# A mixture-of-experts block on one core: the down projection of 25 experts rewritten from eight passes of full width into seven products of half width

## The chip, the core and the metric

The kernel runs on one core of a Trainium2 chip. TensorE (PE in the profile; PEld is its weight load) multiplies matrices into PSUM. VectorE (DVE), ScalarE (ACT) and GpSimd (POOL) do elementwise work. SyncE (SP) issues most DMAs; POOL issues the indirect ones (gathers and scatters by index). The engines run at the same time and wait for one another through semaphores; each works through its own list strictly in the order in which the program wrote it. The metric is the device time of one execution in microseconds (us).

## The reference, cut to what matters

The input is 8 x 1024 tokens of 512 numbers, all in f32. Each token is normalised; one branch is a gated recurrence over time, the other a shared feed-forward block plus 32 routed experts, of which each token uses one. The part that the change touches is the routed branch:

```python
topk_ids = jnp.argmax(logits, axis=-1)
xs = x * scores
sorted_x = xs[order]                       # tokens grouped by expert
g = grouped_mm(sorted_x, routed_gate_w)    # 512 -> 1024, per expert
u = grouped_mm(sorted_x, routed_up_w)      # 512 -> 1024
d = grouped_mm(silu(g) * u, routed_down_w) # 1024 -> 512
out = x + s * silu(shared_out + d[inv])
```

## The kernel before

**Two phases.** The first (to about 2787 us in the profile) runs the recurrence and the shared block over 16 chunks of 512 tokens, with large products in Strassen's form, and routes the tokens. Its last part, the drain, runs only the output projections (L1055). The second phase runs the 32 experts one after the other. Experts are sorted by their number of tokens; the one at place e has a fixed number of slots, `WIDTHS[e]`, from 376 down to 224 (25 of them have 248 or more). Tokens beyond the slots would go to a loop after the experts (L1533), of which the profile has no row.

**One expert** is a `Chunk` (L170). Its slots lie in 2 or 3 tiles of 128 tokens. `gather_in` (L200) fetches token rows with indirect DMAs on POOL, four of 32 rows a tile; `transpose` (L229) turns them on DVE into `xsT`. `compute` (L253) runs over eight blocks j of the hidden size. Per j it does 4 matmuls for g and 4 for u (L272), the sigmoid on ACT (L277), two multiplications on DVE (L279, L280) that give `h`, and then `down` of the block before (L261): 4 matmuls of the full width, which add into four PSUM banks `accs` over all eight j. So gate and up of block j, and down of block j - 1, alternate on PE. At the end DVE transposes the banks (L299) into `yT`.

**What follows an expert** is done during the next one: `store` and `fetch` (L304, L315) take `yT` through DRAM on SP; `gather_rest` (L219) fetches the rows of the other branches; `bias`, `sums` and `finish` (L345, L322, L350) combine them on DVE and ACT; a scatter on POOL writes the output (L360).

**Order.** The order on each engine is written by hand: `between[j]` (L1496 to L1519) lists what is issued after block j. A `gather_in` or weight load of expert e + 2 stands in expert e.

```python
if e + 2 < E:
    between[3 if e == 0 else 1].append(lambda: chunks[e + 2].weight("g"))
    between[2].append(chunks[e + 2].gather_in)
...
between[6].append(chunk.gather_rest)
if e + 2 < E:
    between[7] += [lambda q=q: chunks[e + 2].weight(q) for q in "ud"]
```

**Buffers.** Each weight matrix (2 MB) takes one of NW = 7 buffers in turn (L369). `alloc2` (L376) gives the others: 6 tiles of gathered rows, 3 of `h`, 5 of `rest`. g and u share 4 PSUM buffers, so g of block j + 2 takes the place of g of block j once DVE has read it. The first expert's three matrices are loaded during the drain, each in one DMA, at its start and at steps 10 and 20 (L1460, L1471).

Of the kernel before, what the change touches and what calls it, by code (L numbers as in the profile page):

```python
# [8 lines left out]
FP = mybir.dt.float32  # L9
I32 = mybir.dt.int32  # L10
AF = mybir.ActivationFunctionType
ALU = mybir.AluOpType
# [5 lines left out]
P = 128  # L18
T = 512
NT = T // P  # L20
BL = 32
NA = P // BL
C = 384
CT = C // P
# [9 lines left out]
def tile_kernel(  # L34
# [45 lines left out]
    nc = tc.nc  # L80
    B, S, H = x.shape
    N = B * S
    DI = init_h.shape[0]
    E, _, I = rgate_w.shape
    KH = H // P
    NJ = DI // P
    NI = I // P
# [20 lines left out]
    def work(name):  # L108
        return pools["work"].tile([P, 512], FP, tag="w", name=name)

    pools = {}
# [8 lines left out]
        out=upper, in_=ones, pattern=[[1, P]], compare_op=ALU.is_gt, fill=0.0,  # L120
# [49 lines left out]
    class Chunk:  # L170
# [6 lines left out]
        def __init__(self, alloc, alloc_w, name, cols, fours, width, w_src, whole=False, direct=True):  # L177
            self.whole = whole
            self.direct = direct
            self.alloc, self.alloc_w, self.name, self.w_src = alloc, alloc_w, name, w_src  # L180
            self.width, self.cols, self.fours = width, cols, fours
            self.wt, self.src = [], None
            self.tiles = [
                (t, min(P, width - t * P)) for t in range(-(-width // P))
            ]

        def weight(self, tag):
            q = "gud".index(tag)
            w = self.alloc_w([P, KH * I], f"{self.name}_w{tag}")
            w = w.rearrange("p (k f) -> p k f", k=(KH, KH, NI)[q])  # L190
            self.src = self.src or self.w_src()
            rows = "(k p) f -> p k f" if tag == "d" else "(p k) f -> p k f"
            nc.sync.dma_start(out=w, in_=self.src[q].rearrange(rows, p=P))
            self.wt.append(w)

        def weights(self):
            for tag in "gud":
# [55 lines left out]
        def compute(self, between):  # L253


            wg, wu, wd = self.wt
            xsT, alloc, name, W = self.xsT, self.alloc, self.name, self.width

            def down(j, h):
                for m in range(KH):  # L260
                    nc.tensor.matmul(  # L261
                        accs[m][:, :W], lhsT=wd[:, j, m * P : (m + 1) * P], rhs=h[:, :W],
                        start=(j == 0), stop=(j == NI - 1),
                    )

            last = None
            for j in range(NI):
                g = work(f"{name}_g{j}")
                u = work(f"{name}_u{j}")
                for o, w in ((g, wg), (u, wu)):  # L270
                    for k in range(KH):
                        nc.tensor.matmul(  # L272
                            o[:, :W], lhsT=w[:, k, j * P : (j + 1) * P], rhs=xsT[:, k, :W],
                            start=(k == 0), stop=(k == KH - 1),
                        )
                sig = alloc([P, C], "sig", f"{name}_sig{j}")
                nc.scalar.activation(sig[:, :W], g[:, :W], AF.Sigmoid)  # L277
                h = alloc([P, C], "h", f"{name}_h{j}")
                nc.vector.tensor_tensor(sig[:, :W], sig[:, :W], g[:, :W], ALU.mult)  # L279
                nc.vector.tensor_tensor(h[:, :W], sig[:, :W], u[:, :W], ALU.mult)  # L280
                if last is not None:
                    down(*last)
                last = (j, h)
                for step in between.get(j, ()):
                    step()
            down(*last)
            if self.direct:
                self.yT = alloc([P, KH, C], "yT", f"{name}_yT")
                for m in range(KH):
                    if m % 2:  # L290
                        nc.vector.tensor_copy(self.yT[:, m, :W], accs[m][:, :W])
                    else:
                        nc.scalar.copy(self.yT[:, m, :W], accs[m][:, :W])
                return

            nb = -(-W // BL)
            self.yT = alloc([P, C // BL, KH, BL], "yT", f"{name}_yT")
            for m in range(KH):
                nc.vector.transpose(  # L299
                    self.yT[:, :nb, m, :],  # L300
                    accs[m][:, : nb * BL].rearrange("p (b c) -> p b c", c=BL),
                )

        def store(self):  # L304

# [60 lines left out]
    accs = []  # L366
    ydram = [dram.tile([C, H], FP, name=f"ydram{q}") for q in range(3)]
    yturn = iter(range(E))
    NW = 7  # L369
    turn = iter(range(3 * E))  # L370

    def alloc_w(shape, name):
        i = next(turn) % NW
        return pools["wa" if i < 4 else "wb"].tile(shape, FP, tag=f"w{i}", name=name)

    def alloc2(shape, tag, name):  # L376
        bufs = {"xs": 2 * CT, "xsT": 2, "sig": 2, "h": 3, "y": 3, "s": 2, "yT": 2, "rest": CT + 2}
        pool = pools["in" if tag in ("xs", "xsT") else "by"]
        return pool.tile(shape, FP, tag=tag, name=name, bufs=bufs[tag])

    chunks = [
        Chunk(
            alloc2, alloc_w, f"e{e}",
            lambda t, e=e: pools["idx"][:, e * CT + t : e * CT + t + 1],
            lambda t, b, e=e: pools["fours"][:, b, e * CT + t : e * CT + t + 1],
            WIDTHS[e], lambda e=e: expert(eid[0:1, e : e + 1]), e == 0, e == E - 1,
        )
        for e in range(E)
    ]
# [23 lines left out]
    op = c1.enter_context(tc.tile_pool(name="op", bufs=1))  # L413
# [12 lines left out]
    steps = {}  # L426
# [582 lines left out]
    for c in range(NCHUNK):  # L1009
        g = SC * (c + 1)  # L1010
# [368 lines left out]
    d = Dispatch()  # L1379
# [10 lines left out]
    last = SC * (NCHUNK - 1)  # L1390
# [38 lines left out]
    for now in range(END):  # L1429
        name, back = ORDER[now % 7]  # L1430
        n = now // 7 - back
# [25 lines left out]
    pools["far"] = c1.enter_context(tc.tile_pool(name="far", bufs=2, side="right"))  # L1457
    for _ in range(2):
        out_fetch()
    chunks[0].weight("g")  # L1460
    k = 0
    while filled < 2 * NCHUNK * PER:
        now += 1
        for step in steps.pop(now, ()):
            step()
        while filled < due(now):
            next(fill)
            filled += 1
        k += 1
        if k in (10, 20):  # L1470
            chunks[0].weight("ud"[k // 20])  # L1471
        if filled >= 2 * NCHUNK * PER - 24 and "xsT" not in vars(chunks[0]):
            pools["work"] = ps_w
            for t in range(CT):
                chunks[0].transpose(t)
# [11 lines left out]
    for m in range(KH):  # L1487
        acc = pools["acc"].tile([P, H], FP, tag="acc", name=f"acc{m}")
        nc.vector.memset(acc, 0.0)
        accs.append(acc)  # L1490
    with ExitStack() as c3:
        pools["wb"] = c3.enter_context(tc.tile_pool(name="wb", bufs=1, reuse_waits="tile"))
        pools["by"] = c3.enter_context(tc.tile_pool(name="by", bufs=2, reuse_waits="tile"))
        chunks[1].gather_in()
        for e, chunk in enumerate(chunks):
            between = {j: [] for j in range(NI)}  # L1496
            if e:
                before = chunks[e - 1]
                between[0].append(before.store)
                between[1].append(before.fetch)  # L1500
                for t in range(CT):
                    between[1 + t].append(lambda t=t: before.bias(t))
                    between[3 + t].append(lambda t=t: before.sums(t))
                    between[4 + t].append(lambda t=t: before.finish(t))
            if e == 0:
                for j, tag in enumerate("gud"):
                    between[j].append(lambda tag=tag: chunks[1].weight(tag))
            if e + 2 < E:
                between[3 if e == 0 else 1].append(lambda: chunks[e + 2].weight("g"))
                between[2].append(chunks[e + 2].gather_in)  # L1510
            if e + 1 < E:
                for t in range(CT):
                    between[5 + t].append(lambda t=t: chunks[e + 1].transpose(t))
            between[6].append(chunk.gather_rest)
            if e + 2 < E:
                between[7] += [lambda q=q: chunks[e + 2].weight(q) for q in "ud"]
            if e == E - 1:
                for t in range(CT):
                    between[7].append(lambda t=t: chunk.bias(t))  # L1519
            chunk.compute(between)  # L1520
        for t in range(CT):
            for step in (chunks[-1].sums, chunks[-1].finish):
                step(t)
# [4 lines left out]
    with tc.tile_pool(name="wo", bufs=3) as wo, tc.tile_pool(name="so", bufs=3) as so:  # L1528
        n = nc.values_load(
            nov[0:1, 0:1], min_val=0, max_val=MAXOV,  # L1530
            skip_runtime_bounds_check_because="a sum of at most MAXOV comparisons of counts that sum to N",
        )
        with tc.For_i(0, n, 1) as i:  # L1533
# [5 lines left out]
            def alloc(shape, tag, name):  # L1539
                return so.tile(shape, FP, tag=tag, name=name)  # L1540
# [48 lines left out]
```

## Time and profile before

| what | value |
|---|---|
| median of 3 runs | 4257.02 us (4255.71 to 4257.21) |
| profiled execution | 4237.99 us, of it the span 4236.3 us |
| granted TensorE clock, mean | 0.997 |
| experts 0 to 24 (2786.8 to 3950.8 us): PE busy | 1164.0 of 1164.0 us |
| same stretch: DVE, ACT, POOL busy | 506.5, 122.8, 370.1 us |
| same stretch: DMA engines' mean busy share | 0.65 |
| DVE's waits for the y rows fetched from DRAM | 23.7 us in 19 waits, longest 2.4 |
| DVE's waits for the gathered rest rows | 1.5 us, one wait |

A row of the profile names the line, the engine, the operation and what is written from what; numbers in tile names are left out, so all experts share a row. An f32 matmul is two instructions in the trace, with a weight load (PEld) each. Matmuls are pipelined: the duration of one includes its way through the array, so the distance from start to start, not the duration, tells the rate. Timeline rows give the start, the length, the engine, and in brackets the idle time before and what ended it.

### The profile page before, as it was taken

The numbers are of one execution on the slowest core, as the hardware profiler recorded it, in microseconds if no ns is written. First come the engines' busy times: TensorE is split into PE (matmuls) and PEld (weight loads), VectorE is DVE, ScalarE is ACT, GpSimd is POOL, SyncE is SP. The second block draws the span as 40 slices with busy tenths as digits, with TensorE's granted clock in tenths as the row PEclk, the third lists the DMA queues.
The fourth block names the chain that finished last, engine by engine and source line by source line (L and its number), as shares of the span: only waits on it lengthen the run. The fifth ranks groups of instructions, "written<-read, shape, count | busy, mean of one in ns | idle before, by whom it ended". The sixth has DMA issues, their size and how long they took to land.

```text
span 4236.3 us, 51931 instructions
## 1 busy us (share of the span) xinstructions
PE 4198.9 (99%) x18719; PEld 3527.2 (83%) x18719; DVE 2083.9 (49%) x3425; ACT 1978.0 (47%) x3577; POOL 1105.3 (26%) x1182
## 2 busy tenths in 40 slices
PE   9999999999999999999999999999999999999998
PEld 4688888888888888888888888866777788889998
DVE  5555555544554545555545456424444444544444
ACT  5676676666666766666767666501111111111110
POOL 3222122111221121212211225442232333323221
PEclk9999999999999999999999999999999999999999
DMA  8767666666676666766666656575666567677773
GB/s 277 244 214 231 207 216 216 210 223 206 213 226 216 217 213 203 231 202 216 222 210 220 214 177 205 179 267 181 211 227 226 205 236 242 222 253 242 243 263 113
DMA packets 506854, 925.61 MB, mean 218 GB/s; under 512 B 38397, under 2 KB 324509, under 8 KB 498402
## 3 DMA queue, kind: packets, MB, share of 16 engines
q1 hardware_dynamic: 478754, 831.89, 59.2%
q0 software_dynamic: 27840, 90.36, 6.4%
q8 instruction: 150, 2.46, 0.2%
q14 instruction: 110, 0.90, 0.1%
HBM read 805.27 MB, written 134.92 MB: 222 GB/s over the span
## 4 chain that ended last, share of the span: by engine, by line
PE 97%; DVE 1%; DMA 1%; issue 0%; ACT 0%; POOL 0%; SPq 0%; POOLq 0%; ACTq 0%
PE b L759 24%; PE u L1055 18%; PE c L759 12%; PE e_u L272 11%; PE e_g L272 11%; PE acc L261 11%; PE a L759 6%; PE b L710 3%; PE lgp L520 0%; DMA e_xs<-rec,idx 0%; PE lgt L530 0%; PE b L725 0%; DMA x<-in_L_attn_x_dram 0%; DMA e_rest<-rec,idx 0%; POOL s L1007 0%
## 5 line engine op out<-in xcount | busy, mean ns | idle before, releaser
L759 PE MATMUL b<-t,sums 128*128 128x256 f32 x2400 | 616.1, 379 | 1.2 <-DVE t L681 1.2
L1055 PE MATMUL u<-wP,s 128*128 128x256 f32 x2032 | 598.4, 380 | 6.1 <-issue 6.1
L277 ACT ACTIVATE e_sig<-e_g 128x280 f32<-128x280 f32 (+15 forms) x256 | 101.8, 398 | 931.8 <-PE e_g L272 931.6
L272 PE MATMUL e_u<-e_xsT,e_wu 128*128 128x296 f32 (+15 forms) x2048 | 518.0, 396 | 0.0
L272 PE MATMUL e_g<-e_xsT,e_wg 128*128 128x296 f32 (+15 forms) x2048 | 518.0, 396 | 0.0
L261 PE MATMUL acc<-e_h,e_wd 128*128 128x296 f32 (+15 forms) x2048 | 512.8, 396 | 0.0
L759 PEld LDWEIGHTS b<-t,sums 128*128 128x128 f32 x2400 | 454.8, 190 | 63.0 <-ACT a L773 1.3
L272 PEld LDWEIGHTS e_g<-e_xsT,e_wg 128*128 128x128 f32 x2048 | 389.1, 190 | 87.2
L272 PEld LDWEIGHTS e_u<-e_xsT,e_wu 128*128 128x128 f32 x2048 | 389.1, 190 | 87.1
L261 PEld LDWEIGHTS acc<-e_h,e_wd 128*128 128x128 f32 x2048 | 389.1, 190 | 87.1
L1055 PEld LDWEIGHTS u<-wP,s 128*128 128x128 f32 x2032 | 387.2, 191 | 61.1 <-issue 8.3
L279 DVE TENSOR_TENSOR e_sig<-e_sig,e_g 128x280 f32<-128x280 f32 (+15 forms) x256 | 113.1, 442 | 481.6 <-ACT e_sig L277 481.2
L213 POOL DMA_INDIRECT e_xs<-rec,fours x276 | 262.4, 951 | 178.2 <-DMA e_rest<-rec,idx 86.0
L759 PE MATMUL c<-xnT,sums 128*128 128x256 f32 x1200 | 308.0, 379 | 0.0
L759 PE MATMUL c<-t,sums 128*128 128x256 f32 x1200 | 308.0, 379 | 0.0
L759 PE MATMUL b<-xnT,nat 128*128 128x256 f32 x1200 | 308.0, 379 | 0.0
L759 PE MATMUL a<-xnT,nat 128*128 128x256 f32 x1200 | 308.0, 379 | 0.0
L759 PE MATMUL b<-t,nat 128*128 128x256 f32 x1200 | 308.0, 379 | 0.0
L360 POOL DMA_INDIRECT out_dram<-e_rest,idx x84 | 93.1, 1109 | 801.2 <-DVE e_rest L359 798.2
L759 PEld LDWEIGHTS b<-xnT,nat 128*128 128x128 f32 x1200 | 228.0, 190 | 31.4 <-issue 0.5
L759 PEld LDWEIGHTS a<-xnT,nat 128*128 128x128 f32 x1200 | 228.0, 190 | 31.0
L759 PEld LDWEIGHTS c<-t,sums 128*128 128x128 f32 x1200 | 228.0, 190 | 31.0
(243 smaller groups left out, 6381.2 us busy)
## 6 DMA issues: line engine op xcount, KB each, us to landing
sums<-sdram SPq DMA_DIRECT2D x300, 512.0 KB, 4.6
nat<-in_L_attn_W_dram SPq DMA_DIRECT2D x192, 512.0 KB, 4.6
e_wg<-L_ffn_routed_gate_w_dram SPq DMA_DIRECT2D x32, 2048.0 KB, 8.4
e_wu<-n_L_ffn_routed_up_w_dram SPq DMA_DIRECT2D x32, 2048.0 KB, 12.7
e_wd<-L_ffn_routed_down_w_dram SPq DMA_DIRECT2D x32, 2048.0 KB, 19.0
wP<-tdram SPq DMA_DIRECT2D x127, 512.0 KB, 3.5
nat<-L_ffn_shared_gate_w_dram SPq DMA_DIRECT2D x64, 512.0 KB, 4.9
nat<-n_L_ffn_shared_up_w_dram SPq DMA_DIRECT2D x64, 512.0 KB, 4.3
```

Of the source, the lines that this page charges most:

```text
L213: nc.gpsimd.indirect_dma_start(out=r[:, b, :], out_offset=None, in_=rec1.rearrange("n (a d) -> (n a) d", a=NA), in_offset=bass.IndirectOff ...
L261: nc.tensor.matmul(accs[m][:, :W], lhsT=wd[:, j, m * P : (m + 1) * P], rhs=h[:, :W], start=(j == 0), stop=(j == NI - 1),)
L272: nc.tensor.matmul(o[:, :W], lhsT=w[:, k, j * P : (j + 1) * P], rhs=xsT[:, k, :W], start=(k == 0), stop=(k == KH - 1),)
L277: nc.scalar.activation(sig[:, :W], g[:, :W], AF.Sigmoid)
L279: nc.vector.tensor_tensor(sig[:, :W], sig[:, :W], g[:, :W], ALU.mult)
L360: store = nc.gpsimd.indirect_dma_start(out=of[:, :], out_offset=bass.IndirectOffsetOnAxis(ap=col[:n, :], axis=0), in_=o, in_offset=None, b ...
L710: nc.tensor.matmul(ps[:, part], lhsT=natural[n][:, k, block * P : (block + 1) * P], rhs=xnTs[0][:, k, part], start=(k == 0), stop=(k == KH ...
L759: nc.tensor.matmul(ps, lhsT=lhs[:, k, :], rhs=rhs[:, k, :], start=(new and k == 0), stop=(k == KQ - 1),  skip_group_check=True,)
L1055: nc.tensor.matmul(ps[:, q, :], lhsT=lhs[:, q * P : (q + 1) * P], rhs=w[:, p, :],  start=(q == 0 and p == 0 and name in ("P1", "P2", "P5") ...
```

## The change

For experts with 248 slots or more (and not the last), `down` moves out of the loop over j. The eight `h` blocks are kept in one tile `hid`, and after gate and up of all eight blocks `down_fast` multiplies the 1024 x 512 weights with it in Strassen's form (Winograd's variant): both are cut into four quarters and seven products of quarters replace eight. Each product is 8 matmuls of half the width. The sums of weight quarters (`weight_sum`, 4 of 1024 columns) and of hidden quarters (`down_sum`, 4 of half the width times 4) are new on DVE; ACT copies three intermediate results out of PSUM, DVE adds three, and the result is transposed from a tile `o` in SBUF. The next expert's transposes of its second and third tile move from j = 6, 7 to after the fifth product's eviction, the first to j = 2.

Other edits: weights g and u of expert e + 2, its gather, and then `gather_rest` are issued at j = 7; weight d of expert e + 1 at j = 0, between `store` and `fetch`. The first expert's weights come in four parts of 256 hidden columns, two in the drain (steps 8 and 24), two at j = 0 and 1. NW is 6; there are 3 tiles of gathered rows and 3 of `rest`.

```diff
+            self.fast = not direct and width >= 248
...
+        def quarter(self, q):
+            if q == 0:
+                for tag in "gud":
+                    self.weight(tag, load=False)
+            n, k = I // 4, NI // 4
+            for i, w in enumerate(self.wt[:2]):
+                nc.sync.dma_start(
+                    out=w[:, :, q * n : (q + 1) * n],
+                    in_=self.src[i][:, q * n : (q + 1) * n].rearrange("(p k) f -> p k f", p=P),
+                )
...
+            hid = self.hid = alloc([P, NI, C], "hid", f"{name}_hid")
...
-                if last is not None:
-                    down(*last)
-                last = (j, h)
+                if j and not self.fast:
+                    down(j - 1)
+                if j == NI - 2 and self.fast:
+                    self.down_sum(1)
...
+            if self.fast:
+                self.down_fast(between.get("down", ()))
+            else:
+                down(NI - 1)
...
+        def weight_sum(self, q):
...
+            l, r, op = {
+                1: (A21, A22, ALU.add), 2: (S[:, 0], A11, ALU.subtract),
+                3: (A11, A21, ALU.subtract), 4: (A12, S[:, 1], ALU.subtract),
+            }[q]
+            nc.vector.tensor_tensor(S[:, q - 1], l, r, op)
...
+        def down_fast(self, steps):
+            W, h = self.width, self.width // 2
+            for q in (2, 3):
+                self.down_sum(q)
...
+            for name, ps, lhs, rhs in (
+                ("P1", chain, self.down_part(0, 0), lambda: self.hidden_part(0, 0)),
+                ("P5", side, S[:, 0], lambda: T[1]),
+                ("P6", chain, S[:, 1], lambda: T[2]),
+                ("P2", other, self.down_part(0, 1), lambda: self.hidden_part(1, 0)),
+                ("P7", chain, S[:, 2], lambda: T[3]),
+                ("P3", side, S[:, 3], lambda: self.hidden_part(1, 1)),
+                ("P4", chain, self.down_part(1, 1), lambda: T[4]),
+            ):
+                rhs = rhs()
+                for q in range(2):
+                    for j in range(NI // 2):
+                        nc.tensor.matmul(
+                            ps[:, q * h : (q + 1) * h], lhsT=lhs[:, j, q * P : (q + 1) * P],
+                            rhs=rhs[:, j, :],
...
+                if name == "P1":
+                    evict("a1", ps)
+                elif name == "P5":
+                    evict("b5", ps)
+                    self.down_sum(4)
+                    for step in steps:
+                        step()
...
-    NW = 7
+    NW = 6
...
-        bufs = {"xs": 2 * CT, "xsT": 2, "sig": 2, "h": 3, "y": 3, "s": 2, "yT": 2, "rest": CT + 2}
+        bufs = {"xs": CT, "xsT": 2, "sig": 2, "y": 3, "s": 2, "hs": 2, "rest": CT}
...
-        if k in (10, 20):
-            chunks[0].weight("ud"[k // 20])
+        if k in (8, 24):
+            chunks[0].quarter(k // 24)
...
+    pools["o"] = osb.tile([P, KH, C], FP, name="o")
+    nc.gpsimd.memset(pools["o"], 0.0)
...
+            for q in range(1, 5):
+                between[q + 2 if e == 0 else q - 1].append(lambda q=q: chunk.weight_sum(q))
+            if 0 < e < E - 1:
+                between[0].append(lambda: chunks[e + 1].weight("d"))
             if e + 1 < E:
                 for t in range(CT):
-                    between[5 + t].append(lambda t=t: chunks[e + 1].transpose(t))
-            between[6].append(chunk.gather_rest)
+                    step = (2, "down", "down")[t] if chunk.fast else 5 + t
+                    between.setdefault(step, []).append(lambda t=t: chunks[e + 1].transpose(t))
             if e + 2 < E:
-                between[7] += [lambda q=q: chunks[e + 2].weight(q) for q in "ud"]
+                between[7] += [lambda q=q: chunks[e + 2].weight(q) for q in "gu"]
+                between[7].append(chunks[e + 2].gather_in)
+            between[7].append(chunk.gather_rest)
```

## The prediction, made before the changed kernel ran

> **What bounds the kernel now.** I read the page from the top: busy shares, the slices, then the chain of waits.
>
> ```profile
> PE 4198.9 (99%) x18719; PEld 3527.2 (83%) x18719; DVE 2083.9 (49%) x3425; ACT 1978.0 (47%) x3577; POOL 1105.3 (26%) x1182
> ...
> PE   9999999999999999999999999999999999999998
> ...
> PEclk9999999999999999999999999999999999999999
> ...
> PE 97%; DVE 1%; DMA 1%; issue 0%; ACT 0%; POOL 0%; SPq 0%; POOLq 0%; ACTq 0%
> ```
>
> TensorE (PE) is on the chain for 97% of the span, at full clock. A busy PE need not be a PE at its rate, so I went to its timeline inside the second phase, for an expert of 272 slots:
>
> ```profile
> 3487.27 2.00 PE L272 MATMUL e_g<-e_xsT,e_wg 128*128 128x272 f32 x8
> 3489.11 2.00 PE L272 MATMUL e_u<-e_xsT,e_wu 128*128 128x272 f32 x8
> ...
> 3494.61 2.00 PE L261 MATMUL acc<-e_h,e_wd 128*128 128x272 f32 x8
> ```
>
> Each f32 matmul is two records, so 4 matmuls show as x8. Starts are 1.835 us apart: 229.3 ns a record. Expert 0 (376 slots) begins at 2786.79 and expert 1 at 2847.43: 60.64 us for 192 records, 315.8 ns each. Both fit (columns / 1.2 + 2.5) ns. With it the 25 experts of 248 slots or more (widths sum to 7200) take 192 x (6000 + 25 x 2.5) ns = 1164.0 us; the trace has expert 25 start at 3950.79, 1164.00 us after 2786.79. PE has no gap there: what saves PE records saves time, and any wait put before PE costs in full.
>
> **The records saved.** Down was 64 records of the full width W. Strassen has 7 products x 8 matmuls = 112 records of W/2. In W, 64W/1.2 - 56W/1.2 = 6.67W ns is saved, less 48 x 2.5 = 120 ns: 1.69 us at W = 272. Over 25 experts 48.0 - 3.0 = 45.0 us, if 124 to 188 columns keep the same rule. No row has such a matmul with these operands, and PEld speaks against it:
>
> ```profile
> L261 PEld LDWEIGHTS acc<-e_h,e_wd 128*128 128x128 f32 x2048 | 389.1, 190 | 87.1
> ```
>
> If a load's 190 ns were its pitch, 112 records would take 21.3 us at every width: 25 x 21.3 = 532 us against 64 x (6000 + 62.5) ns = 388 us now, 144 us lost. The Trainium skill, "TensorE: Matmul & The Clock Gate", section LDWEIGHTS, prices a load at columns/1.2, 107 ns for 128. Two small places decide: a pair of loads with little to hide behind, and four transposes of 128 columns.
>
> ```profile
> 2520.70 0.29 PEld L1205 LDWEIGHTS terms<-terms,ones 32*128 32x128 f32 x2 [0.33 <-issue]
> ```
>
> ```profile
> 416.48 0.60 PE L530 MATMUL lgt<-ident,lgT 128*128 128x128 f32 x4
> 416.92 0.81 PE L759 MATMUL b<-t,sums 128*128 128x256 f32 x3
> ```
>
> The two loads, 0.18 us each, fit into 0.29: the second starts 0.11 after the first. The four transposes, each with its own load, start 0.11 apart, which is 128/1.2 + 2.5. So 190 is a latency and about 108 ns the floor. The same page's section "Back-to-back issue gap" says more against the change: sustained pairs at 128 columns take about 81 ns where the plain formula gives 56, 25 ns more. By that rule 2800 records x 25 ns = 70 us would turn 45 saved into 25 lost. The transposes show no such excess, and I take the trace. Only 124 columns (105.8 ns) fall under 108: 3 experts x 112 x 2.7 ns = 0.9 us. **Saved on PE: 44.1 us** (1164.0 to 1119.9). The seven products wait on other engines; a satisfied wait costs nothing in the present rows.
>
> **DVE, the engine that must now keep up.** Gate and up no longer have down between them: a step j lasts 16 records, 3.67 us at 272, where it was 5.50. These are DVE's intervals now:
>
> ```profile
> 3511.31 0.44 DVE L280 TENSOR_TENSOR e_h<-e_sig,e_u 128x272 f32<-128x272 f32 x1 [0.47 <-PE e_u L272]
> 3511.66 0.68 DVE L357 TENSOR_TENSOR e_rest<-e_rest 128x512 f32<-128x512 f32 x1
> 3512.38 0.69 DVE L358 TENSOR_TENSOR e_rest<-e_rest,e_s 128x512 f32<-128x512 f32 x1
> 3513.11 0.69 DVE L359 TENSOR_TENSOR e_rest<-e_rest 128x512 f32<-128x512 f32 x1
> 3513.71 0.69 DVE L339 TENSOR_TENSOR e_rest<-e_y,e_rest 128x512 f32<-128x512 f32 x1
> ```
>
> Start to start: the pair of mults 0.79, 512 columns 0.60, finish 0.72 + 0.73 + 0.60 = 2.05, a transpose 1.09. New: a weight sum of 1024 columns, nearest row L905 (1214 ns), and a hidden sum of 4 x 136 = 544, 0.73 from the 512 row. With them:
>
> - j2: 0.79 + bias 0.60 + weight sum 1.21 + transpose 1.09 = 3.69
> - j3: 0.79 + sums 0.60 + bias 0.60 + weight sum 1.21 = 3.20
> - j4 and j5: 0.79 + finish 2.05 + sums 0.60 = 3.44 each
> - j6: 0.79 + hidden sum 0.73 + finish 2.05 = 3.57
>
> 17.3 us of DVE in 18.3 of PE. At 264, the tightest, 17.2 in 17.8. DVE just fits. Call the end of u7 T. DVE does the last mult and the second hidden sum by about T + 1.4; P1 and P5 (32 records of 115.8 ns) cover until T + 3.7, where P6 needs that sum. So a lag of DVE up to **2.3 us is free**; beyond that PE stands. P4 needs P7's add, with P3 (1.85 us) as cover for 0.6: free. Evictions by ACT (0.4 us each, ACT at a tenth here) are covered by the product between. The fourth hidden sum waits for P5; behind it on DVE stand two transposes for the next expert, done by T + 6.3, needed at T + 13.
>
> **Queues that are moved.** POOL: the gather of e+2 now stands at j7 ahead of gather_rest, and its second tile waits for those transposes. At 1.25 us a gather, rest0 is issued at T + 12.1. DVE wants it (bias in j1, behind it all of j2) at about T + 20.8. Landing has these bounds: 5.1 us with no weights under way (last expert, 4207.34 to 4212.45) and
>
> ```profile
> e_rest<-rec,idx POOLq DMA_INDIRECT x84, 10.9
> ```
>
> with 4 MB of weights beside it. Here gate and up (4 MB) start at T and are nearly through at T + 13, so I take 7 to 8: no stall; both ends stay inside the free lag (10.9 gives a lag of 2.2).
> SP: weight d (2 MB) now stands between the y stores and the y fetch. Without weights yT to landing took 6.2 us (last expert); a 2 MB load adds some 6.4 (8.4 to landing for e_wg, less 2). From yT at S + 1.7 (S = next expert's start) that is S + 14.3; sums(0) is reached at S + 15.1. With the gathers sharing the DMA it may be 1 us late, inside the free lag. Six weight buffers leave gate and up of e+2 a whole expert of time, down as well.
>
> **The first expert.** Here PE stood for 6.06 us, because DVE waited for number DMAs that shared the DMA engines with 4 MB of weights, and P5 waited for the add behind it:
>
> ```profile
> 2766.87 0.41 DVE L1338 TENSOR_SCALAR fours<-number,piece 128x372 int32<-128x372 f32 x1 [3.15 <-DMA number<-table]
> ...
> 2768.54 0.68 DVE L1067 TENSOR_TENSOR o<-u,a 128x512 f32<-128x512 f32 x1
> ...
> 2769.33 5.83 PE L1055 MATMUL u<-wP,s 128*128 128x256 f32 x16 [6.06 <-issue]
> ```
>
> Now 1.5 MB is ahead of them. Gain between 0 and 6.1; I take **3**. Parts 3 and 4 are issued near PE's start of expert 0 and wanted 20 and 30 us later: free. The POOL memset delays gathers that have 15 us: free. The seven narrow experts keep form and cover.
>
> **Sum.** The profiled run took 4238.0 (span 4236.3 and 1.7 around it). 4238.0 - 44.1 - 3 + 2 (short waits at P6 in the experts of 264 to 280) = 4192.9. The median of the runs lies 19.0 above the profiled run; carried over: **4212 us**.
>
> **Rivals.**
> - DVE as the bound, still faster (0.22): with DVE 10 to 20% slower than these intervals the lag passes 2.3 by 1 us or so in most three-tile experts, about 20 x 1 us: 4232. For it: 17.2 of 17.8. Against: rows, not guesses, make up most of the sum.
> - The rest gather late (0.10), **slower**: for a landing of L us DVE stands L - 8.7, PE that less 2.3, in each of 25 experts. It eats the gain (44.1/25 = 1.8) at L = 12.8. At L = 15 (the longest of any rest or scatter DMA is 15.3): 4.0 x 25 = 100 us, 4310. For it: a third tile beside weights took 13.3 us (3205.97 to 3219.25). Against: the weights are mostly in.
> - Short matmuls don't reach the rule (0.04): 4280 by the 25 ns, 4398 by 190.
> - The waits together give back just the gain (0.05): 4257.
>
> **Chances.** The forecast 0.59, 4205 to 4222; with the DVE rival, faster is 0.81. A change within 0.2% (8.5 us) can't be told from none: 0.05. Slower 0.14. The range runs from nearly all of the gain and the gap to half of it: 4204 to 4250.
>
> **What would show it.** PE records of down at W/2/1.2 + 2.5 ns (115.8 at 272); an expert of 272 lasting 42.3 instead of 44.0; idle of PE before P6 near zero; DVE's idle before bias and before sums on DMA under a microsecond each; the gap near 2763 halved. The forecast is wrong if P6 or g4 waits for DVE every expert, or if loads set the records' pitch.

## The result, and the profile after

| | before | after |
|---|---|---|
| median | 4256.56 us (4255.71 to 4257.21) | 4403.4 us (4379.1 to 4406.25) |
| ratio, 95% interval | | 1.0337 (1.0319 to 1.0355) |
| profiled execution | 4237.99 us, span 4236.3 | 4403.59 us, span 4401.8 |
| experts 0 to 24 | 1164.0 us | 1316.1 us |

The change made the kernel 3.4% slower; forecast was 4212. This size holds for some sets of runs only. Each set below has the kernel before beside it on the same chip. In four sets the kernel before took about 4240 us, and the changed one, in the three of them where it ran, 1.010 times that; in three sets (the first is one) the kernel before took 4253 to 4260, and the changed one, in the two where it ran, about 4390 to 4403. I call them quiet and disturbed sets. They differ in one thing that the traces show, told further down.

The page of the changed kernel (first, disturbed set); the parts shown are busy time, slices, granted clock and the chain:

```profile
PE 4214.4 (96%) x19919; PEld 3606.8 (82%) x19919; DVE 2285.4 (52%) x3700; ACT 2011.7 (46%) x3677; POOL 1110.0 (25%) x1183
...
PE   9999999999999999999999999998989988889997
...
PEclk9999999999999999999999999999999999989999
...
PE 1%; issue 0%; DMA 0%; DVE 0%; POOL 0%; POOLq 0%; DVEq 0%
```

PE's busy time is up only 15 us, and its last third has slices under 90%: it waits there. The chain of waits breaks off after 1%, because semaphore records are missing (10,164 after 2780 us, where a quiet set's trace of the same kernel has 14,695), so it can't be read. The list of waits can, here of the changed kernel's second phase (who waited for whom: us in total, times, longest):

```profile
PE acc L392 <- DVE o L417: 75.9, 13, 9.6
PE acc L392 <- issue: 36.5, 17, 9.3
...
DVE o L417 <- remote: 178.9, 31, 9.5
```

L392 is a product of `down_fast`, L417 the adds of P2, P7 and P3. PE waits for DVE's add, and DVE for something that the profile can't name ("remote"). Expert 4's tail, from the timelines of DVE and PE:

```profile
3063.46 0.49 DVE L417 TENSOR_TENSOR o<-acc,e_a 128x320 f32<-128x320 f32 x1 [4.98 <-PE acc L392]
3071.96 0.49 DVE L417 TENSOR_TENSOR o<-acc,e_b 128x320 f32<-128x320 f32 x1 [8.01 <-remote]
...
3060.26 4.51 PE L392 MATMUL acc<-e_hid,e_ws 128*128 128x160 f32 x32
3072.51 4.03 PE L392 MATMUL acc<-e_hs,e_wd 128*128 128x160 f32 x16 [7.75 <-DVE o L417]
```

The 32 records are P7 and P3. P7's end at 3062.6, yet DVE, idle, starts P7's add at 3071.96, and P4 needs that add. A stall costs twice. From the windows view (length, busy time and records of PE, PEld, DVE, ACT, POOL, granted clock, DMA share, GB/s):

```profile
3062.00:3066.00 4.00, 2.77 (x21) 2.52 (x19) 0.49 (x1) 0.00 (x0) 2.84 (x4) 1.00 0.32 98
3066.00:3070.00 4.00, 0.00 (x0) 0.00 (x0) 0.00 (x0) 0.00 (x0) 2.76 (x3) 0.87 0.66 185
3070.00:3074.00 4.00, 1.49 (x5) 1.49 (x6) 1.79 (x4) 0.00 (x0) 0.00 (x0) 0.50 0.92 307
```

While PE idles its granted clock falls to 0.50, and P4 takes 3.9 us from start to start where its rule gives 2.2. Only POOL works there: it issues gathers.

### The profile page after: what moved, and what is told of

It reads as the page before. It is cut to its first block, busy times and chain, and to the rows that moved or that the text cites. A ratio compares the mean times of both kernels' runs of the same rounds, so it can differ in the third digit from the quotient of the medians.

```text
span 4401.8 us, 54915 instructions
## 1 busy us (share of the span) xinstructions
PE 4214.4 (96%) x19919; PEld 3606.8 (82%) x19919; DVE 2285.4 (52%) x3700; ACT 2011.7 (46%) x3677; POOL 1110.0 (25%) x1183
## 5 line engine op out<-in xcount | busy, mean ns | idle before, releaser
L291 PE MATMUL e_g<-e_xsT,e_wg 128*128 128x296 f32 (+15 forms) x2048 | 531.4, 403 | 14.3 <-DVE e_sig L297 13.5
L874 PEld LDWEIGHTS b<-t,nat 128*128 128x128 f32 x1200 | 228.0, 190 | 31.0
L874 PEld LDWEIGHTS c<-xnT,sums 128*128 128x128 f32 x1200 | 228.0, 190 | 31.0
L890 ACT ACTIVATE u<-b,vec 128x256 f32<-128x256 f32 x360 | 171.6, 477 | 174.2 <-PE b L874 173.5
```

Of the source, the lines that this page charges most:

```text
L291: nc.tensor.matmul(o[:, :W], lhsT=w[:, k, j * P : (j + 1) * P], rhs=xsT[:, k, :W], start=(k == 0), stop=(k == KH - 1),)
L874: nc.tensor.matmul(ps, lhsT=lhs[:, k, :], rhs=rhs[:, k, :], start=(new and k == 0), stop=(k == KQ - 1),  skip_group_check=True,)
L890: nc.scalar.activation(o, ps, AF.Identity, bias=bias(n, block))
```

## Where the time goes, by set

For experts 0 to 24, the distance between starts less (columns/1.2 + 2.5) ns for each record; that rule alone gives 1119.0 us. Split by place:

| kernel (set) | over the rule | before P4 | P4 at a low clock | before P6 | gate and up, rest | experts 25 to 30 |
|---|---|---|---|---|---|---|
| before | 0.0 | | | | 0.0 | 0.0 |
| changed, first (disturbed) | 197.1 | 107.4 | 28.7 | 4.4 | 56.6 | 11.0 |
| changed, after_again (quiet) | 81.8 | 0.0 | 0.4 | 21.6 | 59.9 | 11.8 |
| rest_first (quiet) | 8.2 | 0.0 | 0.4 | 5.3 | 2.5 | 7.6 |
| combined (quiet) | 3.4 | 0.0 | 0.4 | 0.6 | 2.4 | 0.0 |
| combined_third (disturbed) | 161.2 | 44.4 | 17.5 | 0.6 | 98.7 | 6.2 |
| g_early_again (disturbed) | 47.6 | 1.7 | 0.6 | 9.1 | 36.3 | 10.6 |

So there are two losses: one of some 82 us in the quiet sets, at P6 and in gate and up, and one at P4 that only disturbed sets have. What the disturbed sets lose in gate and up is not the quiet loss over again. In the first trace VectorE waits 9.9 us in all for the rest gathers up to 4200 us, and not once before expert 26; in after_again it is 144.7 us. Expert 10, with 5.4 us one of the largest losses there, starts late because ScalarE (ACT) sees the end of expert 9's P4 some 10 us after it (P4 ends at 3346.2):

```profile
3356.29 0.41 ACT L411 COPY o<-acc 128x296 f32<-128x296 f32 x1 [17.67 <-remote]
```

The experiments take the two apart.

## The experiments

**One part undone at a time** (quiet set, the kernel before at 4239.73). First the weights away from j7, the gathers left there:

```diff
-                between[0].append(lambda: chunks[e + 1].weight("d"))
+                for j, tag in zip((3, 3, 3), "gud"):
+                    between[j].append(lambda tag=tag: chunks[e + 1].weight(tag))
...
-                between[7] += [lambda q=q: chunks[e + 2].weight(q) for q in "gu"]
```

> Against the changed kernel only the weight loads move: the 4 MB of gate and up that stand at j7 ahead of ten gathers (and the 2 MB of down at j0 of the next expert) are issued together at j3 of the next expert; the gathers stay at j7. Theory A (TensorE's completion signals to DVE come up to 9 us late while indirect gathers are issued into a DMA system that is busy with 4 MB of weights): the 8 to 10 us before P4 go, 4205 to 4240 us. Theory B (a row of thirteen gathers on POOL alone holds DVE up): 4380 to 4410, as the changed kernel. Theory C (the short matmuls of Strassen's form outrun their own signals): 4380 to 4410.

Measured 4219.02, ratio 0.9958 (0.9942 to 0.9974): 0.4% faster than before. Then the gathers written at j0, the weights left:

```diff
+                between[0].append(chunks[e + 1].gather_in)
...
-                between[7].append(chunks[e + 2].gather_in)
...
-                    step = (2, "down", "down")[t] if chunk.fast else 5 + t
+                    step = ("down" if e else (2, "down", "down")[t]) if chunk.fast else 5 + t
```

> Against the changed kernel the ten gathers of the inputs move from j7 to j0 of the next expert (its transposes all stand in the down part), the weights stay at j7 with the three gathers of the rest. Theory A: the long waits before P4 go, since little is gathered beside the 4 MB; 4210 to 4270 (2 MB of down weights still meet the gathers). Theory B: the stalls move with the row of gathers into gate and up, 4330 to 4400. Theory C: 4380 to 4410.

Measured 4209.48, ratio 0.9927 (0.9911 to 0.9944). Its trace shows what the edit really did: nothing holds POOL at j0, so the ten gathers follow right behind the three of the rest, 9 to 15 us after P1's start in the three-tile experts. It put the rest gathers first. And Strassen's form switched off (`self.fast = False`):

> The changed kernel with Strassen's form switched off in every expert: all down projections are the plain interleaved 64 records; the order of loads and gathers, the buffers and the first expert's parts stay as changed. Theory A: the late signals stay and hit the pairs g and u, which have about one step (5.5 us) of slack: 4270 to 4340, slower than the kernel before. Theory B: about the same, 4270 to 4340. Theory C: no late signals, 4240 to 4260, as the kernel before.

Measured 4253.26, ratio 1.0033 (1.0021 to 1.0044), below what A and B gave. No signal was late in any of the three traces, so theories A, B and C, which are all about late signals, were not tested here; that 4219 falls inside A's range was luck. But VectorE waits for the rest gathers here too, and for longer than anywhere else:

```profile
DVE e_rest L463 <- DMA e_rest<-rec,idx: 243.2, 59, 8.5
```

PE loses 0.7 us in experts 0 to 24, in which 187.6 us of these waits lie: with down between the steps, DVE has 5.5 us for a step instead of 3.7 and catches up. (Most of what plain_down lost is in the narrow experts 25 to 30, 9.7 us.) So the late rest comes with the new order of loads and gathers, and moving down behind gate and up takes its cover away.

**The changed kernel again, and what in the tail matters** (quiet set, the kernel before at 4240.01).

> The changed kernel once more, beside the next three. Theories P and D below: 1.03 times the kernel before, some 4370 to 4410 us, with completion signals of TensorE up to 9 us late in the trace. Theory X (the first runs met a disturbed chip, since the plain down with the same loads and gathers showed no late signal): 4190 to 4220.

Measured 4285.57, ratio 1.0105 (1.0088 to 1.0122): in between, slower than before but with every signal on time.

```diff
-            nc.vector.tensor_tensor(S[:, q - 1], l, r, op)
...
+            self.hs[q] = (B12, B22, B12, B21)[q - 1]
+            return
...
```

> The changed kernel without the eight sums on VectorE: the four sums of down weights and the four of hidden parts are left out and the products read plain parts instead, so the output is not the reference's; products, evictions, adds, loads and gathers stay. Theory P (the short matmuls with their dense weight loads are what makes the signals late once loads and gathers meet): stalls as in the changed kernel, 4350 to 4400. Theory D (sums of two SBUF operands on VectorE, beside POOL's gathers, make them late): 4190 to 4215.

Measured 4247.19, ratio 1.0012 (1.0005 to 1.0019): neither. VectorE's waits for the rest stay (149.6 us in 33 waits), but with less to do it catches up sooner: 44.9 us over the rule instead of 81.8, none of it at P6.

```diff
-                self.down_fast(between.get("down", ()))
+                for q in (2, 3, 4):
+                    self.down_sum(q)
+                for j in range(NI):
+                    down(j)
+                for step in between.get("down", ()):
+                    step()
...
```

> The changed kernel with the plain 64 matmuls of full width behind gate and up in place of the seven products; the eight sums on VectorE are still made, though nobody reads them; evictions and adds are gone. Theory P: no late signals, 4235 to 4260. Theory D: late signals and missing semaphore records in the trace, 4260 to 4330.

Measured 4293.83, ratio 1.0123 (1.0106 to 1.014); no late signal, but 48.3 us over its rule. And the same with matmuls of half the width, without sums:

> The changed kernel with the plain down behind gate and up, each matmul cut into two of half the columns (128 of W/2 in place of 112), without sums, evictions and adds. Theory P: late signals and missing semaphore records in the trace; its time some 4270 to 4340, since fewer waits stand behind the signals than in the changed kernel. Theory D: no late signals, 4240 to 4265 (128 x 2.5 ns - 64 x 2.5 ns = 0.16 us an expert more than plain).

Measured 4276.92, ratio 1.0084 (1.0067 to 1.0101); no late signal, 24.7 us over. P and D were theories of the late signals, and this set had none, so neither was tested. What the two show is that the loss needs no product of Strassen's: down behind gate and up, with the new order of loads and gathers, is enough. Where does it come from? Expert 11 of the quiet run of the changed kernel, POOL's timeline and then DVE's (P1 starts at 3376.58):

```profile
3375.53 1.20 POOL L475 DMA_INDIRECT out_dram<-e_rest,idx  x1 [3.47 <-DVE e_rest L474]
3384.97 0.89 POOL L475 DMA_INDIRECT out_dram<-e_rest,idx  x1 [8.24 <-DVE e_xsT L267]
3386.16 1.01 POOL L232 DMA_INDIRECT e_xs<-rec,fours  x1 [0.30 <-issue]
...
3397.49 0.94 POOL L242 DMA_INDIRECT e_rest<-rec,idx  x1 [0.30 <-issue]
...
3399.72 0.45 DVE L298 TENSOR_TENSOR e_hid<-e_sig,e_u 128x280 f32<-128x280 f32 x1 [1.00 <-PE e_u L291]
3406.64 0.69 DVE L463 TENSOR_TENSOR e_rest<-e_rest,b2b 128x512 f32<-128x512 f32 x1 [6.48 <-DMA e_rest<-rec,idx]
```

The second scatter of the previous expert leaves at 3375.53, just behind the issue of weight g at 3374.89. The third scatter writes the same output and waits for the second to land. Its sequencer passes that wait at 3384.11, 8.6 us after the issue; the row names the transposes because they ended last (3384.84), but the data that it stores was finished at 3380.5. Then come nine gathers, and the first rest gather leaves 20.9 us after P1's start. DVE needs it, stands for 6.48 us, and is late for g, u and P6 through most of the expert. The late DVE finishes the next expert's tiles late, so its second scatter again leaves behind the weights: the loss keeps itself alive. In experts 3 to 6 the second scatter leaves 4.3 us or more before P1 and lands in 3 to 4 us, the rest leaves 14.4 to 15.1 us after P1, and the experts have exactly the rule's length; from expert 7 to 20 all but one are in the late state, and expert 21 (it stores expert 20, which has two tiles and so no third scatter) ends it.

What starts it is another queue. In expert 7 DVE stands for the y rows fetched from DRAM, and its finish of expert 6 comes after them:

```profile
3164.99 0.69 DVE L454 TENSOR_TENSOR e_rest<-e_y,e_rest 128x512 f32<-128x512 f32 x1 [2.53 <-DMA e_y<-ydram]
```

The second scatter then leaves 2.3 us before P1 instead of 4.3, 0.5 us before weight g, and takes 9.0 us to land. In experts 3 to 6 the same wait was 0.5 to 0.9 us. The other two quiet traces of the changed kernel enter the late state the same way, after a wait for y of 2.7 us (after_fourth, expert 7) and of 2.1 and then 3.1 us (after_third, experts 5 and 6). In w_later, where no weights stand at j0, the longest such wait up to expert 24 is 0.6 us; since it moved the other loads too, that weight d ahead of the fetch makes y late is likely but not shown alone.

**The rest first** (quiet set, the kernel before at 4240.29), one swap against the changed kernel:

```diff
+            between[7].append(chunk.gather_rest)
+            if e + 2 < E:
                 between[7].append(chunks[e + 2].gather_in)
-            between[7].append(chunk.gather_rest)
```

> The changed kernel with one swap: at j7 the gathers of the rest (three) go before those of the inputs (ten). Theory G (in the three-tile experts POOL holds a scatter until the scatter before it has landed behind 4 MB of weights, and the rest gathers wait behind it and behind ten input gathers until 21 us after u7; VectorE then waits some 7 us for them and TensorE for VectorE): rest gathers go out within 9 us after u7, the wait for them on VectorE is gone in the experts with Strassen's form, 4210 to 4230. Theory V (VectorE's own load is too much in a step of 16 records): no change, 4275 to 4295. Where the late completion signals of the first run come back, 100 us or so more in either theory.

Measured 4208.44, ratio 0.9926 (0.9909 to 0.9942), as theory G says. The same expert, POOL and DVE (P1 at 3359.59):

```profile
3355.94 1.19 POOL L475 DMA_INDIRECT out_dram<-e_rest,idx  x1 [3.46 <-DVE e_rest L474]
3361.21 0.89 POOL L475 DMA_INDIRECT out_dram<-e_rest,idx  x1 [4.09 <-DVE e_rest L474]
3362.40 1.09 POOL L242 DMA_INDIRECT e_rest<-rec,idx  x1 [0.30 <-ACT e_a L378]
...
3381.05 0.68 DVE L463 TENSOR_TENSOR e_rest<-e_rest,b2b 128x512 f32<-128x512 f32 x1
```

The rest leaves 2.8 us after P1's start and the bias add runs without idle time. Where the third scatter is still held (experts 16, 18, 19, 20: 6.7 to 7.9 us after P1), the rest leaves by 9.1 and is in time: a held scatter alone does no harm, nor do ten gathers alone; together they do.

**All in one**: weights at j3 as in w_later, the rest first, and `if k in (30, 32)` for the first two quarters.

> Three edits to the changed kernel: all three weights of an expert are loaded at j3 of the expert before it, the gathers of the rest go before those of the inputs, and the first two quarters of the first expert's weights are issued some 10 us later, behind the number loads. Theory G: no waits but small ones at P6; the narrow experts at the end run without waits too: 4195 to 4210. The gap near 2763, if the quarters held the number loads up: 2 to 4 us in place of 5.2 to 6.3; if not, unchanged. Theory V: 4270 to 4290.

Measured 4196.41, ratio 0.9898 (0.9882 to 0.9915): 1% faster than before. The list of waits has one for PE in the second phase, 0.5 us long, at the very end.

**The changed kernel once more**, in that set and in another quiet one with the kernel before at 4240.11:

> The changed kernel a third time, to see which of its two times comes back: 1.010 times the kernel before, with no late completion signal in the trace, or 1.034, with TensorE's signals up to 9 us late. If the late signals belong to the chip, the kernel before stands at 4256 beside them and at 4240 without.

> The changed kernel a fourth time: what was first measured (4403 us, TensorE's signals up to 9 us late, the kernel before at 4256) may belong to the chip that it ran on. If this call meets that chip, the kernel before stands near 4256 and this one near 4400 with late signals; otherwise near 4240 and 4280 without.

> The combined kernel once more beside it. Where the signals of TensorE come on time: 4193 to 4200. On a chip where they come late while loads and gathers meet: since its gathers leave POOL with no weights under way, the signals should stay on time and the time within 20 us of 4196; if they come late here too, the meeting of loads and gathers is not the condition, and 4240 to 4330 is to be seen.

Measured 4282.27, ratio 1.0097 (1.008 to 1.0113); 4286.1, ratio 1.0109 (1.0079 to 1.0138); and 4195.75, ratio 0.9895 (0.9867 to 0.9924).

**Two disturbed sets.** One execution each, beside 4252.99 before:

> The changed kernel, looked at once more beside the next. On a chip or at a time like the first (the kernel before near 4256): some 4400 us, signals of TensorE late. Else 4280 to 4290.

> The kernel with the input gathers at j0, where 4 MB of weights meet three gathers and 2 MB meet ten. If this call meets late signals in the changed kernel: on time here if it takes the long row of gathers beside 4 MB (4210 to 4230), late here too if any gather beside weights is enough (4250 to 4350). Else 4205 to 4212, which tells nothing new.

Measured 4390.62 with late signals as in the first trace, and 4249.85. Then, with 4259.64 before, the combined kernel and one with this edit against the changed kernel (and the later quarters):

```diff
-                between[0].append(lambda: chunks[e + 1].weight("d"))
+                between[0].append(chunks[e + 1].gather_in)
+                for tag in "gud":
+                    between[4].append(lambda tag=tag: chunks[e + 1].weight(tag))
...
-            if e + 2 < E:
-                between[7] += [lambda q=q: chunks[e + 2].weight(q) for q in "gu"]
-                between[7].append(chunks[e + 2].gather_in)
```

> The changed kernel with the ten input gathers at j0 of the next expert, all three weights of an expert at j4 of the expert before it, only the three rest gathers at j7, and the first two quarters later. On a chip with signals on time (the kernel before near 4240): 4193 to 4205. On a chip where a row of gathers makes signals late (before near 4253): nothing stands in the tail but three gathers, so 4230 to 4255, as with the gathers at j0.

> The combined kernel (thirteen gathers in the tail, rest first, no weights under way there). On a chip with signals on time: 4193 to 4200. On the other: if the row of gathers alone makes the signals late, P4 waits for P7's add again, 4290 to 4360; if it takes 4 MB of weights beside the row, 4200 to 4230.

Measured 4348.98, ratio 1.021 (1.018 to 1.024), against the 4230 to 4255 that I gave; and 4365.53, ratio 1.0249 (1.0219 to 1.0279). Spread doesn't do what its text says: as in g_early nothing holds POOL at j0, and the ten gathers run in the tail. In the combined kernel no weights are under way in the tail, and P4 waits all the same, as PE's timeline of expert 2 shows:

```profile
2947.80 4.58 PE L392 MATMUL acc<-e_hid,e_ws 128*128 128x168 f32 x31
2959.36 0.93 PE L392 MATMUL acc<-e_hs,e_wd 128*128 128x168 f32 x2 [6.97 <-DVE o L417]
```

So late signals need no weights beside the row of gathers. A count says it more sharply. I took every PE matmul that signals a semaphore in the second phase, and asked whether its signal is on record within 0.3 us of its end, inside a row of at least five gathers (to 2.6 us past its last) and outside:

| trace | late or missing inside rows | outside |
|---|---|---|
| changed, first (disturbed) | 129 of 215 | 2 of 516 |
| combined_third (disturbed) | 137 of 223 | 0 of 507 |
| g_early_again (disturbed) | 143 of 247 | 5 of 483 |
| changed, after_again (quiet) | 0 of 286 | 0 of 445 |
| combined (quiet) | 0 of 285 | 0 of 444 |

In seven experts of the first trace P7's add starts 2.40 to 2.59 us after the last gather's end. What a late signal costs depends on who waits. In g_early_again the row starts 9 us or later after P1 in the three-tile experts (the rest gathers hold it up) and lies mostly beside the next expert's gate and up, where PE has two steps of PSUM buffers ahead: 36.3 us there, 1.7 before P4. In the other two it covers P2, P7 and P3, each of which hands over to DVE with about 2 us to spare.

## Why the prediction was wrong

It was wrong in sign. In the first set, and the other disturbed one that has the changed kernel, the step that failed is the one at P4; in the quiet sets it is the issue of the rest. Point by point:

- **PE's saving: right.** A tail at 272 columns, combined kernel, from PE's timeline:

```profile
3530.44 2.02 PE L392 MATMUL acc<-e_hid,e_wd 128*128 128x136 f32 x16
3532.30 3.87 PE L392 MATMUL acc<-e_hs,e_ws 128*128 128x136 f32 x32
3536.00 2.02 PE L392 MATMUL acc<-e_hid,e_wd 128*128 128x136 f32 x16
```

 16 records in 1.86 us, 116 ns each, against 115.8 forecast. The 25 ns that the Trainium skill ("TensorE: Matmul & The Clock Gate", section Back-to-back issue gap) puts on sustained pairs doesn't show: it would make 141. The floor was mis-sized: 128 and 124 columns both run at 111.6 ns (12.50 us for 112 records), not 108, so the three experts of 248 lose 0.65 us each instead of 0.3 (0.2 by its own 108, which is 2.2 ns over 105.8, not 2.7), and two of 256 lose 0.27. In the combined kernel experts 0 to 24 take 1122.4 us, a saving of 41.6 where I had 44.1.
- **DVE just fits: right, while nothing holds it.** Sizes held (a weight sum 1.22 us, hidden sums 0.73 at 280), and in the combined kernel 0.6 us is lost before P6 over all 25 experts. But "free lag 2.3 us" left no room for a wait of 6 us, and a DVE loaded to 17 in 18 us can't make one up within an expert.
- **"P4 needs P7's add, with P3 as cover for 0.6: free": this is the step that failed in the disturbed sets, and so in the first.** The sum put nothing for it. In the first trace the wait before P4 is 107.4 of the 197.1 us over the rule, and P4 at a low clock 28.7 more, because the signal from P7 to its add comes up to 9 us late while a row of gathers is issued. In quiet sets the P4 column is 0.0. The profile before could not show it: its trace has every signal on time. So most of the 3.4% comes from late signals, of which the prediction had no trace.
- **"rest0 is issued at T + 12.1": this is the step that failed in the quiet sets.** T is u7's end, some 0.2 us before P1's start. In after_again it went out 14.4 to 15.1 us after P1 in experts 3 to 6 and about 20 to 23 us after it in 13 of the 14 from 7 to 20. I counted the ten gathers and the wait for the transposes, but not the third scatter ahead of them, which waits for a scatter's landing behind the 4 MB that the change issues at the same point. The rival "rest gather late" named the place and the chain (rest, bias, DVE, PE), and its 4310 is near the 4283 of the quiet sets; it looked for the cause in the landing, which was 9.2 us at most in expert 11, 0.5 over its free 8.7. I gave it 0.10. In the first trace this step cost nothing up to expert 25: the rest left 13.4 to 15.9 us after P1 in 15 of the 19 three-tile experts from 1 on (18.5 to 20.9 in the others), and DVE, held up by late signals itself, did not wait for it.
- **SP's queue: wrong in the quiet sets.** I allowed y's fetch to be 1 us late, inside the free lag. It cost DVE 35.7 us in 13 waits in after_again's second phase up to expert 29 (23.7 in 19 before), and PE next to nothing directly; but in each of the three quiet traces a wait of 2.5 to 3.1 us is what pushes the second scatter back to the weights, and from there on the rest is late.
- **The gap near 2763: wrong.** I took 3 us of 6.06, blaming the 4 MB ahead of the number loads. It stayed at 5.0 to 6.3 us in the changed kernel's five traces, and at 5.7 in the combined kernel, where the quarters come behind those loads:

```profile
2759.21 0.53 POOL L1452 DMA_DIRECT2D number<-table  x1 [1.40 <-DMA e_xs<-rec,idx]
...
2765.73 0.42 DVE L1453 TENSOR_SCALAR fours<-number,piece 128x372 int32<-128x372 f32 x1 [2.98 <-DMA number<-table]
```

 From the last number load's issue to its use are 6.5 us without the weights ahead, and 6.7 with them (rest_first, and before). So the weights are not what makes this load long; I take it that what counts is when POOL gets to issue it, which no run changed alone.
- **The 19 us from profile to median** were no property of the kernel but of the set: the profile belongs to a quiet one (4238), the times to a disturbed one (4257). From profile to profile the sum gave 4192.9; the combined kernel's profiled execution took 4195.2. That they lie so close is in part luck: the 2 us for P6 and the 3 for the gap were both not met. The saving was there. In the quiet sets the new order of loads and gathers took more than it back; in the disturbed ones late signals did, and no order that was tried is shown to have won it back.

**What stays open.** Why signals are late while POOL issues gathers in some sets and never in others: the chip, its neighbours or the moment. No run changed that at will. The quiet sets ran on chips 3, 4 and 9 (9 twice), the two later disturbed ones on chips 6 and 10; that no chip shows both speaks for the chip, but with one set on each of 6 and 10 it doesn't show it. Nor is it known whether POOL's issuing or the traffic of the gathers is what delays the signals, since the one never ran without the other. Whether the kernel before loses its 13 to 20 us in disturbed sets in the same way isn't known, as none of its traces is from one. And no version here was shown to be faster than before in a disturbed set: g_early came nearest with one execution of 4249.85 beside 4252.99, too few to tell. A row of gathers held back until the middle of an expert wasn't tried.

## What to carry to other kernels

Before moving a step on an in-order queue, list everything between the waiting instruction and the one that is needed, with what each waits for: here a store that waited for another store's landing, behind newly issued weights, held a row of twelve gathers. A place in a program's order is not a time: a DMA issued "at j0" runs as soon as its queue is free. And interleaved work is a cover: taking it out to save engine time exposes waits that it hid (187.6 us of DVE's waits cost PE 0.7 us in plain_down).

## What the runs showed of the hardware

- While POOL issues indirect DMAs 1.25 us apart, the completion signals of TensorE (VectorE's and ACT's too: in the first trace 61 of 203 and 21 of 76 inside such rows, 1 of 1044 and none of 367 outside) can reach the waiting engine up to 9 us late, some of them only 2.4 to 2.6 us after the last gather. Three of seven sets had it.
- A scatter that POOL issued at most 0.5 us ahead of 4 MB of weights, or up to 2.4 us behind the first of them, landed in 8.4 to 9.0 us (after_again, the second scatters of experts 7 to 20 but one); 1.1 us or more ahead of them it took 2.8 to 3.9 (experts 1 to 6 and 15).
- An idle of 8 us costs TensorE about 1.7 us more through its granted clock of 0.50 afterwards (P4 in 3.9 instead of 2.2 us). The Trainium skill ("TensorE: Matmul & The Clock Gate", section What's actually happening) says that activity releases the throttle; the windows rows agree.
- In the disturbed traces some matmuls also start 0.7 or 1.4 us after the one before, where 0.23 is the rule, with no semaphore to wait for and at a granted clock of 1.00; for instance six times between 3592.6 and 3599.0 in combined_third. Six quiet traces (before, after_again, w_later, g_early, rest_first, combined) have no such pause in the second phase.
